# Two weighted sums in another loop order, two half steps of a value projection between three score products, and a key projection cut into a matmul part and a split part

## The chip, the cores and the metric

The kernel runs on 1 core of a Trainium2 chip, as one program. The metric is the device time of one execution in microseconds (us). Three executions of the kernel before took 3112.5, 3117.52 and 3116.73 us; their median is 3116.73 us.

## What is computed

The input is x of shape (4, 256, 64, 64), float32: four images of 256 channels and 4096 points. Two layers follow each other. The reference, cut to what matters here:

```python
# layer 0: self-attention over the 4096 points of an image
q, k, v = wq @ xf + bq, wk @ xf + bk, wv @ xf + bv      # 32, 32 and 256 channels
attn = softmax(q.T @ k);  x = gamma * (v @ attn.T) + x
# layer 1: clustering block
feat, val = conv1x1(group_norm(x), f_w), conv1x1(group_norm(x), v_w)   # 4 heads of 24, 4 folds
sim = sigmoid(beta + alpha * cos(centres, points))       # 4 centres for each fold and head
sim = sim * one_hot(argmax(sim, over the centres))
agg = (sim @ val + pooled val) / (count + 1)             # the weighted sums
y = x + ls1 * conv1x1(agg spread back by sim, proj)
y = y + ls2 * mlp(group_norm(y))                         # 256 -> 1024 -> gelu -> 256
z = relu(bn(conv1x1(relu(bn(y * dw)), pw)))
```

## The kernel before

**Stages.** The images are worked on one after another (b = 0 to 3, line 2061). For each, three functions run: `weighting` (line 958, exponentials and weighted values of the attention, 64 units of 512 keys by 512 queries), `cluster` (line 1141, the clustering block up to the statistics of the second group norm) and `mlp` (line 1639, MLP and pointwise convolution). The scores of the next image's first 8 units are computed inside `cluster` and `mlp` of the present one, so that the next `weighting` can start at once.

**Order of the work.** The program is under a manual schedule: each engine executes its instructions in the order in which the Python code issues them, and semaphores hold an instruction until its inputs are there. TensorE (PE) thus has one hand-written queue, as have VectorE (DVE), ScalarE (ACT), GpSimd (POOL) and the DMA queue on SyncE (SP).

**Fill.** The projections of the next image are cut into a list of small pieces (`parts.projections`, lines 1130 to 1134), each with a size. `fill(n)` (line 2048) pops pieces from this list until their sizes add up to n. It is called at places where PE would otherwise wait. A value piece, `v_step(i, k)` (line 437), has size 1/2 and is one matmul of 128x128 weights by 256 columns, which the hardware executes as two passes. Two values of i share one PSUM buffer of the pool `ps_m`, and the last of their four pieces lets ACT copy the buffer to SBUF (line 451). The list is: values 0 to 13, the first key projection, values 14 to 31, then the second key and the second query projection, each with size 1. That is 35 in sizes. In the first three images the calls to `fill` use up 30 of them before the early scores, 1 and 2 more in the second group norm, so that the second key and query projections are left for `fill(N)` (line 1966), behind the first of the MLP's hidden pieces, `first(0, 0)`.

**Key and query projections.** `halved` (line 425) runs `projected` (line 346: 8 matmuls of 128x32 weights by 512 columns, in turn into the four 32-row quarters of a PSUM buffer), then `halves_of` (line 359), which splits the float32 result into a rounded part (ACT, line 368) and a rest (DVE, line 369), and then sends both to DRAM with four DMAs of SP.

**Early scores.** At the end of `cluster` three units are scored one after another (lines 1516 to 1519). Each `score` (line 539) has four matmuls of 512 columns into two PSUM buffers of the pool `ps_s`, which has just two, and two ACT copies of 128x1024 (line 502).

**Weighted sums.** `summed` (line 1369) is called twice in `cluster`: with the constant `pool_w` as weights (line 1390), and with `sim` as weights (line 1401). Each call has 32 matmuls of 128x32 weights by 96 columns. They go into the four 32-row quarters of one PSUM buffer (q = 0 to 3), and the 8 chunks of points (j) are added up in PSUM. The loop over j is outside, that over q inside, so that consecutive matmuls write four different quarters in turn. Between the two calls stands `fill(5)`, or `fill(4)` in the last image. `weights(0)` and `weights(1)` (line 1285) on DVE write the part of `sim` that belongs to q = 0 and 1, and to q = 2 and 3. Behind the second call come the counts (line 1406), a copy of the sums by ACT (line 1407), transposes (lines 1417 and 1426), the product with the projection (line 1439), and from it the matmuls `op` (line 1461), whose results DVE adds to y (line 1473). DVE then takes the statistics (line 1454), which feed the second group norm.

**Second group norm.** `group_norm` (line 301) has two tiny matmuls (lines 309 and 310), `fill(1)`, a third matmul (line 320), ACT's square root (line 224), a table load for the gelu (line 299), and `fill(counts)`. Its default for `counts` is 2. Then `norm(0)` normalises the first 512 points on DVE (lines 1672 and 1739 to 1742), and `first(0, 0)` starts the MLP on PE (line 1859).

Of the kernel before, what the change touches and what calls it, by code (L numbers as in the profile page):

```python
# [10 lines left out]
AF = mybir.ActivationFunctionType  # L11
# [22 lines left out]
EARLY = 3  # L34
# [26 lines left out]
def attention_then_cluster_block(  # L61
# [235 lines left out]
    def table(f):  # L297

        nc.scalar.activation(probe, probe, f)
# [38 lines left out]
    def attention(b, xs, ys):  # L338
# [7 lines left out]
        def projected(which, i, ps):  # L346

            col = 1 if which == "k" else 0
            for k in range(KC):
                for r in range(RG):  # L350
                    nc.tensor.matmul(
                        ps[r * D : (r + 1) * D],
                        wqk_s[:, k, col],
                        block(xs, k, 4 * i + r),
                        start=(k == 0),
                        stop=(k == KC - 1),
                    )

        def halves_of(which, hi, lo, ps):

            col = 1 if which == "k" else 0
            if which not in own:
                own[which] = dram.tile([NBLK // RG, P, 4, NB], F32, tag=which, name=f"{which}_{b}")
            bias = bqk_s[:, col : col + 1]
            nc.scalar.activation(hi, ps, AF.Identity, bias=bias)
            nc.vector.scalar_tensor_tensor(
                lo, ps, bias, hi.bitcast(F32), ALU.add, ALU.subtract  # L370
            )

        def part_of(which, c, hi, lo):
            return (hi if c in ((0, 2) if which == "k" else (0, 1)) else lo).bitcast(F32)

        def written(which, i, hi, lo, dma=nc.sync):
            rows = own[which][i]
            for c in range(4):
                dma.dma_start(out=rows[:, c], in_=part_of(which, c, hi, lo))
# [42 lines left out]
                ks[u], ks[u + 1] = two[:, 0], two[:, 1]  # L422
            straight("k", u % RG, ks[u], *src)

        def halved(which, i, write=True):

            ps = ps_m.tile([P, NB], F32, tag="m", name=f"{which}p_{b}_{i}")
            two = work.tile([P, 2, NB], F32R, tag="t13", name=f"hl_{which}_{b}_{i}")
            projected(which, i, ps)
            halves_of(which, two[:, 0], two[:, 1], ps)  # L430
            if write:
                written(which, i, two[:, 0], two[:, 1])
            return two[:, 0], two[:, 1]

        vps = {}
# [689 lines left out]
        parts = Parts()  # L1125
# [5 lines left out]
            (1 / KC, lambda i=i, k=k: v_step(i, k)) for i in range(N // P) for k in range(KC)  # L1131
        ]
        parts.projections[14 * KC : 14 * KC] = [(1, lambda: halved("k", 0))]
        parts.projections += [(1, lambda w=w: halved(w, 1)) for w in "kq"]
        parts.queries = lambda: halved("q", 0)
        return parts

# [3 lines left out]
    def cluster(b, ys, stats, cells, rest, fill, gelu, nxt, maxima, turn):  # L1141
# [112 lines left out]
        def similar(f, between=lambda: None):  # L1254

            def meanwhile():
                table(AF.Gelu_apprx_tanh)
                between()

            sg = sgs[f]  # L1260
            rsqrt(prns[f], prns[f], L2_EPS, meanwhile)
            nc.vector.tensor_tensor(quad(sg), quad(sg), over_m(prns[f]), ALU.mult)
            nc.scalar.activation(sg, sg, AF.Tanh, scale=ab[:, 0:1], bias=ab[:, 1:2])
            if f == 0:
                gelu(0)
                table(AF.Sqrt)
# [24 lines left out]
        later = {6: lambda: similar(0)}  # L1291
# [30 lines left out]
        for nb in range(NBLK):  # L1322
# [7 lines left out]
            ps = ps_s.tile([P, 2, 2, C], F32, tag="s", name=f"fv_{b}_{nb}")  # L1330
# [19 lines left out]
            for g in range(2):  # L1350
                q = 2 * fh + g
# [15 lines left out]
        agg_p = ps_a.tile([P, NB], F32, tag="a0", name=f"agg_{b}")  # L1367

        def summed(w, first):
            for j in range(8):  # L1370
                for q in range(4):
                    nc.tensor.matmul(
                        agg_p[q * 32 : (q + 1) * 32, :ED],
                        w(j, q),
                        vf[2 * (q // 2) + j // 4][:, (j // 2) % 2, 2 * (q % 2) + j % 2, ED:],
                        start=(first and j == 0),
                        stop=(not first and j == 7),
                    )
# [70 lines left out]
        stats2 = small.tile([P, 2 * NBLK, 6], F32, tag="stats", bufs=1, name=f"st2_{b}")  # L1449
# [66 lines left out]
        for u in range(EARLY):  # L1516
            copies = []
            nxt.score(u, copies, maxima)
            copies.pop()()
        return stats2  # L1520


# [116 lines left out]
    def mlp(b, ys, stats2, fill, nxt, blocks, turned, maxima):  # L1639
# [16 lines left out]
        w3_s, (pw_bcd, pw_bac, pw_abcd) = few[:, :h_n], (few[:, h_n + i] for i in range(3))  # L1656
        nc.gpsimd.tensor_tensor(w3_s, s2_s, a12_s, ALU.add)
        ga, gb = group_norm(
            b, "gn2", stats2, fill, meanwhile=lambda: table(AF.Gelu_apprx_tanh)
        )  # L1660
        ob = out[b].rearrange("(k p) h w -> p k (h w)", p=P)
        pairs = {}
# [145 lines left out]
        def first(nb, j, todo, slots, meanwhile=lambda: None):  # L1808


            hs = work.tile([P, 2, NB], F32, tag=("t", "acc")[j % 2], bufs=1, name=f"hs_{b}_{nb}_{j}")

            def gelu(i, src):
                nc.scalar.activation(  # L1814
                    src, src, AF.Gelu_apprx_tanh, bias=pvc("b1", P, j + 4 * (i > 1))
                )

            ws = [
                w[:, j * P : (j + 1) * P] for w in (W_A, w_abcd, W_CD, w_bac, w_bcd, W_B, W_D)
            ]  # L1820
            seven(f"{nb}_{j}", ws, pairs[nb][:, 0], pairs[nb][:, 1], quarters(hs), gelu, todo, slots, meanwhile)
            return hs
# [120 lines left out]
        def rest():  # L1943
            if maxima:
                maxima.pop(0)()
# [8 lines left out]
        for nb in range(blocks):  # L1954
            end = nb == blocks - 1
            for j in range(4):
                if j > 1:
                    rest()
                if end and j == 3:

                    rest()
                    rest()
                pw = (lambda: last(nb - 1, True, nc.gpsimd)) if end and j == 2 else lambda: None
                hs = first(nb, j, todo, slots, pw)
                if nb == 0 and j == 0:
                    fill(N)
                if j > 1 or end:
                    rest()
                if nxt and nb:
                    for _ in range(3 if end else 1):  # L1970
                        if nxt.sums:
                            nxt.sums.pop(0)()
                if j == 0:
                    if nb:
                        rectify = finish(nb - 1, acc)
                    acc = [
                        ps_a.tile([P, NB], F32, tag=f"a{c}", name=f"mo{c}_{b}_{nb}")
                        for c in range(KC)
                    ]
                    if not end:  # L1980
                        acc += [
                            ps_m.tile([P, NB], F32, tag="m", name=f"mo{c}_{b}_{nb}")
                            for c in range(2, 4)
                        ]
                    elif nxt:

                        nc.sync.dma_start(
                            out=a21_s, in_=w2.rearrange("(k p) m -> p k m", p=P)[:, :h_n, P:]
                        )
                        nxt.q_block(1)  # L1990
                elif j == 1:
                    assert not drips and not hooks
                    if nb:
                        rectify()
                    if not end:
                        ahead = norm(nb + 1, nc.gpsimd)
                        if nb:
                            own = factors(nc.gpsimd, pairs[nb - 1][:, 1], pairs[nb - 1][:, 0])
                        else:
                            own = left_factors()  # L2000
                elif j == 2 and nb and not end:
                    pointwise(nb - 1)
                scored = nxt and (nb, j) in at
                if scored:
                    copies = []
                    nxt.score(at[nb, j], copies, maxima)
                    copies.pop()()
                if len(acc) == KC:
                    todo = second(nb, acc, hs, j)
                    slots = (2, 1, 0, 1) if scored else (0, 1, 1, 2)  # L2010
                else:
                    todo = second_by_seven(nb, acc, hs, j, own, ahead)
                    slots = (0, 2, 2, 3)
                    if scored:
                        slots = (3, 1, 2, 1)
                    elif j == 2 and nb:
                        slots = (3, 1, 0, 3)
# [38 lines left out]

    with tc.manual_schedule():
        here = attention(0, xs0, [])
        here.alone()
        late = None  # L2060
        for b in range(B):
            xs1 = []
            nxt = attention(b + 1, xs1, []) if b + 1 < B else None
# [10 lines left out]
            fill = filler(todo)  # L2074
# [11 lines left out]
            stats2 = cluster(b, here.ys, stats, cells, rest, fill, gelu, nxt, maxima, turn)  # L2086
# [79 lines left out]
```

## Time and profile before

The profiled execution took 3112.69 us; its span on the core is 3110.9 us. So 1.8 us lie around the span. The mean granted clock of TensorE was 0.998 of full speed.

| engine | busy us | share of the span | instructions |
|---|---|---|---|
| PE (matmul) | 3042.2 | 98% | 14210 |
| PEld (weight load) | 2488.0 | 80% | 14210 |
| DVE | 2501.5 | 80% | 3548 |
| POOL | 2327.7 | 75% | 2243 |
| ACT | 1779.4 | 57% | 2817 |

The span is one sequence of four images of about 760 us each. In the table a matmul counts as busy until its modelled end, and matmuls overlap, so 98% does not say that the array is always at its peak. Timeline rows give the start in us from the beginning of the span, the time from the first start to the last end of a merged group, the engine, the line, the operation, the tiles (out<-in), the shape and the number of instructions; a bracket at the end tells how long the engine idled before, and what ended the idle time. One float32 matmul of the program appears as two matmul records with two weight loads; the two passes are counted one by one in the rows.

### The profile page before, as it was taken

Reading aid. Unit: us, or ns where it says so; the run is one execution under the profiler, and the core shown is the slowest. Engines: PE = TensorE matmul, PEld = TensorE weight load, DVE = VectorE, ACT = ScalarE, POOL = GpSimd, SP = SyncE. Lnnn points to the kernel's source line nnn. Section 1 sums busy time; section 2 is a strip of 40 time slices with the busy share of each in tenths; the row PEclk is TensorE's granted clock in tenths of the full one; section 3 lists DMA queues with packets and bytes.
Section 4 is the critical chain, followed back from the end, with each engine's and each line's share of the span. In section 5 each row is a group of like instructions: output and inputs, shape, how many; then the busy total and the mean of one; then the engine's idle time right before and its main releaser. Section 6 shows DMA issues by size and latency. Waiting matters only on the chain.

```text
span 3110.9 us, 41355 instructions
## 1 busy us (share of the span) xinstructions
PE 3042.2 (98%) x14210; PEld 2488.0 (80%) x14210; DVE 2501.5 (80%) x3548; ACT 1779.4 (57%) x2817; POOL 2327.7 (75%) x2243
## 2 busy tenths in 40 slices
PE   8999999999999999999999999999999999999999
PEld 5788887788688888878868888887877888885886
DVE  4998888777798888877779888877768988887675
ACT  5666664544566666454456666645456666655444
POOL 6888887477588888648758888965766988894563
PEclk9999999999999999999999999999999999999999
DMA  5112226100112113510011222441011212150000
GB/s 175 45 58 65 62 84 176 58 18 28 52 45 68 55 62 108 159 48 28 18 58 45 69 62 65 117 147 35 28 41 48 59 54 68 55 154 2 13 21 28
DMA packets 105570, 200.40 MB, mean 64 GB/s; under 512 B 14880, under 2 KB 30864, under 8 KB 103824
## 3 DMA queue, kind: packets, MB, share of 16 engines
q1 hardware_dynamic: 100464, 178.66, 18.0%
q0 software_dynamic: 4256, 18.90, 2.9%
q8 instruction: 113, 1.85, 0.2%
q14 instruction: 97, 0.79, 0.1%
q10 hardware_dynamic: 640, 0.20, 0.0%
HBM read 147.01 MB, written 48.34 MB: 63 GB/s over the span
## 4 chain that ended last, share of the span: by engine, by line
PE 74%; DVE 9%; POOL 8%; issue 3%; ACT 3%; DMA 2%; SPq 1%; POOLq 0%; ACTq 0%; DVEq 0%
PE av L734 34%; PE mo L1776 10%; PE sc L489 7%; PE hq L1859 5%; PE hp L1859 3%; PE hr L1859 3%; PE fv L1334 3%; POOL acc L664 3%; DVE s L655 2%; POOL t L664 2%; DVE top L513 2%; PE vp L443 1%; POOL s L664 1%; PE mo L1760 1%; DMA w<-in_w 1%
## 5 line engine op out<-in xcount | busy, mean ns | idle before, releaser
L502 ACT COPY s<-sc 128x1024 f32<-128x1024 f32 x512 | 515.1, 1012 | 427.5 <-PE sc L489 419.0
L655 DVE TENSOR_TENSOR s<-s,hold 128x1024 f32<-128x1024 f32 x512 | 598.4, 1209 | 10.7 <-ACT hold L638 5.5
L664 POOL TENSOR_TENSOR acc<-acc,t 128x512 f32<-128x512 f32 x408 | 541.4, 1347 | 0.0
L734 PE MATMUL av<-s,sum 128*128 128x256 f32 x2048 | 526.9, 380 | 3.7 <-POOL s L664 3.5
L734 PE MATMUL av<-t,v 128*128 128x256 f32 x2048 | 527.1, 380 | 2.4 <-POOL t L664 2.2
L734 PE MATMUL av<-s,v 128*128 128x256 f32 x2048 | 525.7, 379 | 2.2 <-ACT xn L1727 1.1
L664 POOL TENSOR_TENSOR s<-t,s 128x512 f32<-128x512 f32 x256 | 340.5, 1330 | 226.3 <-DVE t L678 158.9
L678 DVE TENSOR_TENSOR t<-s,hold 128x1024 f32<-128x1024 f32 x256 | 311.7, 1218 | 189.8 <-POOL acc L664 93.3
L513 DVE TENSOR_TENSOR top<-sc,top 128x1024 f32<-128x1024 f32 x350 | 426.6, 1219 | 21.6 <-ACT s L502 18.0
L734 PEld LDWEIGHTS av<-s,v 128*128 128x128 f32 x2048 | 387.2, 189 | 64.6 <-ACT xn L1727 2.3
L734 PEld LDWEIGHTS av<-t,v 128*128 128x128 f32 x2048 | 387.5, 190 | 63.1 <-POOL t L664 8.4
L734 PEld LDWEIGHTS av<-s,sum 128*128 128x128 f32 x2048 | 387.9, 190 | 61.1 <-POOL s L664 8.6
L1814 ACT ACTIVATE hs<-hs,pv_s 128x256 f32<-128x256 f32 x496 | 232.6, 503 | 352.3 <-DVE hs L1850 352.3
L489 PE MATMUL sc<-q,k 128*128 128x512 f32 x1024 | 391.6, 466 | 22.2 <-ACT s L502 10.5
L1776 PE MATMUL mo<-hs,w 128*128 128x256 f32 x1512 | 384.9, 381 | 0.0
L664 POOL TENSOR_TENSOR t<-s 128x512 f32<-128x512 f32 x256 | 329.8, 1288 | 45.4 <-PE av L734 31.9
L1776 PEld LDWEIGHTS mo<-hs,w 128*128 128x128 f32 x1512 | 283.6, 190 | 47.2 <-ACT hs L1814 6.3
L659 ACT ACTIVATE hold<-s 128x512 f32<-128x512 f32 x256 | 154.2, 602 | 214.4 <-DVE s L655 214.2
L1850 DVE TENSOR_TENSOR hs<-hq,hs 128x256 f32<-128x256 f32 x496 | 198.5, 421 | 85.8 <-PE hq L1859 75.5
L661 ACT ACTIVATE s<-s 128x1024 f32<-128x1024 f32 x256 | 266.9, 1043 | 0.0
L489 PEld LDWEIGHTS sc<-q,k 128*128 128x128 f32 x1024 | 173.7, 189 | 110.9 <-DVE top L513 59.1
L734 PE MATMUL av<-t,sum 128*128 128x256 f32 x1024 | 262.4, 378 | 0.0
(292 smaller groups left out, 4844.2 us busy)
## 6 DMA issues: line engine op xcount, KB each, us to landing
k<-k SPq DMA_DIRECT2D x248, 256.0 KB, 2.7
x<-in_x SPq DMA_DIRECT2D x62, 512.0 KB, 6.8
out<-xn SPq DMA_DIRECT2D x62, 256.0 KB, 2.1
att<-t SPq DMA_DIRECT2D x56, 256.0 KB, 4.0
x<-att POOLq DMA_DIRECT2D x12, 1024.0 KB, 9.7
w<-in_w SPq DMA_DIRECT2D x8, 1024.0 KB, 11.4
q<-q SPq DMA_DIRECT2D x31, 256.0 KB, 4.1
rden<-row_rd SPq DMA_DIRECT2D x28, 256.0 KB, 3.7
```

The costliest lines, as they stand in the source:

```text
L489: nc.tensor.matmul(sc[:, r, :], k_s[:, (2 * h + r) * P : (2 * h + r + 1) * P], qs[u // GRP], start=True, stop=True,)
L502: nc.scalar.copy(slots[u][:, PAIR[h]].rearrange("p h r n -> p r h n"), tiles(sc))
L513: nc.vector.tensor_tensor(top, src, top if saved[nb] is None else saved[nb], ALU.max)
L655: nc.vector.tensor_tensor(sh, sh, mb.to_broadcast([P, 2, 2, QW]), ALU.subtract)
L661: nc.scalar.activation(s[:, PAIR[1]], s[:, PAIR[1]], AF.Exp)
L664: nc.gpsimd.tensor_tensor(out, x, y, op)
L678: nc.vector.tensor_tensor(t31[u], s[:, B11 : B22 + 1 : 2], b12.to_broadcast([P, 2, 2, QW]), ALU.add)
L734: nc.tensor.matmul(av[bank][:, half_ * QW : (half_ + 1) * QW], a[:, r], t[:, r], start=(g == 0 and r == 0 and i in (1, 7, 2, 4)), stop=(g ...
L1776: return nc.tensor.matmul(bank[:, half * HB : (half + 1) * HB], a[:, j], t, start=start, stop=stop)
L1814: nc.scalar.activation(src, src, AF.Gelu_apprx_tanh, bias=pvc("b1", P, j + 4 * (i > 1)))
L1850: nc.vector.tensor_tensor(dst, ps, term, ALU.add)
L1859: nc.tensor.matmul(out, w, x, start=True, stop=True)
```

## The change

The diff in full:

```diff
@@ -422,14 +422,23 @@
+        ripe = []
+
-        def halved(which, i, write=True):
+        def halved(which, i, write=True, later=False):
 
             ps = ps_m.tile([P, NB], F32, tag="m", name=f"{which}p_{b}_{i}")
             two = work.tile([P, 2, NB], F32R, tag="t13", name=f"hl_{which}_{b}_{i}")
             projected(which, i, ps)
-            halves_of(which, two[:, 0], two[:, 1], ps)
-            if write:
-                written(which, i, two[:, 0], two[:, 1])
+
+            def split():
+                halves_of(which, two[:, 0], two[:, 1], ps)
+                if write:
+                    written(which, i, two[:, 0], two[:, 1])
+
+            if later:
+                ripe.append(split)
+            else:
+                split()
             return two[:, 0], two[:, 1]
@@ -1131,7 +1140,8 @@
-        parts.projections += [(1, lambda w=w: halved(w, 1)) for w in "kq"]
+        parts.projections += [(1, lambda w=w: halved(w, 1, later=w == "k")) for w in "kq"]
+        parts.ripe = ripe
@@ -1367,8 +1377,8 @@
         def summed(w, first):
-            for j in range(8):
-                for q in range(4):
+            for q in range(4):
+                for j in range(8):
                     nc.tensor.matmul(
                         agg_p[q * 32 : (q + 1) * 32, :ED],
                         w(j, q),
@@ -1517,6 +1527,8 @@
             copies = []
             nxt.score(u, copies, maxima)
             copies.pop()()
+            if u + 1 < EARLY:
+                fill(0.5)
         return stats2
@@ -1656,7 +1668,12 @@
         ga, gb = group_norm(
-            b, "gn2", stats2, fill, meanwhile=lambda: table(AF.Gelu_apprx_tanh)
+            b,
+            "gn2",
+            stats2,
+            fill,
+            meanwhile=lambda: table(AF.Gelu_apprx_tanh),
+            counts=2,
         )
@@ -1963,6 +1980,8 @@
                 hs = first(nb, j, todo, slots, pw)
                 if nb == 0 and j == 0:
+                    if nxt:
+                        nxt.ripe.pop(0)()
                     fill(N)
```

- **Sums:** in `summed` the loop over the quarter q is now outside and that over the chunk j inside. The 8 matmuls of one quarter follow each other, 16 passes in a row into the same quarter. This holds for both calls in all four images.
- **Half steps:** between the three early scores of the first three images `fill(0.5)` is called twice. It runs the two pieces of value 29, one behind score 0 and one behind score 1; the second of them is followed by ACT's copy of values 28 and 29.
- **Second keys:** the list of pieces is thereby one size further on in the second group norm. Its `fill(1)` runs value 30, and its `fill(2)` value 31 and the matmuls of the second key projection. ACT's and DVE's split of these keys and their four DMAs are put off until behind `first(0, 0)`, where they stood before too. `fill(N)` then has only the second query projection left.
- `counts=2` is what the default gave.

## The prediction

> **What bounds the kernel now.** I read the page first: engine shares and the chain of work that ended last.
>
> ```profile
> PE 3042.2 (98%) x14210; PEld 2488.0 (80%) x14210; DVE 2501.5 (80%) x3548; ACT 1779.4 (57%) x2817; POOL 2327.7 (75%) x2243
> ...
> PE 74%; DVE 9%; POOL 8%; issue 3%; ACT 3%; DMA 2%; SPq 1%; POOLq 0%; ACTq 0%; DVEq 0%
> ```
>
> PE bounds nearly everything, so PE time in a dense stage is paid in full, and whatever moves into a PE wait is free. The change touches some 45 us of each image, where the chain also runs through DVE and ACT. So I took the timeline by engine there. First the weighted sums of image 0: PE, then ACT, then the last image.
>
> ```profile
> 565.11 1.53 PE L1372 MATMUL agg<-vf,pool_w 128*32 128x96 f32 x64
> 566.57 4.58 PE L443 MATMUL vp<-wv_s,x 128*128 128x256 f32 x20
> 571.08 0.36 PE L1372 MATMUL agg<-vf,sim 128*32 128x96 f32 x4
> 572.44 1.51 PE L1372 MATMUL agg<-vf,sim 128*32 128x96 f32 x60 [1.00 <-DVE sim L1287]
> ...
> 574.10 0.60 PE L1417 MATMUL tp<-ident,sim 128*128 128x128 f32 x4
> ```
> ```profile
> 574.00 0.24 ACT L1407 COPY scr<-agg 128x96 f32<-128x96 f32 x1 [1.58 <-PE agg L1372]
> ```
> ```profile
> 2848.46 1.86 PE L1372 MATMUL agg<-vf,sim 128*32 128x96 f32 x64
> ```
>
> Each sum is 64 passes. PE runs the first, then fill, then 4 passes of the second (q = 0 and 1 of the first chunk), then waits 1.00 us for `weights(1)`. ACT waits for the end of the sum. Then DVE:
>
> ```profile
> 578.17 2.73 DVE L1473 SCALAR_TENSOR_TENSOR x<-op,pc_s,x 128x512 f32<-128x512 f32 x4 [2.45 <-PE op L1461]
> 580.81 2.46 DVE L1454 BATCH_NORM_STATS2 st<-x 128x6 f32<-128x512 f32 x4
> 583.19 2.71 DVE L1473 SCALAR_TENSOR_TENSOR x<-op,pc_s,x 128x512 f32<-128x512 f32 x4
> 585.82 7.20 DVE L1454 BATCH_NORM_STATS2 st<-x 128x6 f32<-128x512 f32 x12
> 593.05 0.59 DVE L307 BATCH_NORM_AGGREGATE mv_gn<-st 128x2 f32<-128x96 f32 x1
> ```
>
> From 578.17 to 593.64 DVE has no gap, and it began because PE's `op` came, which hangs on the sum by way of ACT's copy. So a sum that ends later delays the group norm, and with it the MLP, one to one. Last, the scores, the norm and the start of the MLP, on PE and ACT:
>
> ```profile
> 588.29 1.28 PE L489 MATMUL sc<-q,k 128*128 128x512 f32 x4
> 590.21 0.74 PE L489 MATMUL sc<-q,k 128*128 128x512 f32 x2 [0.63 <-ACT s L502]
> 591.12 0.74 PE L489 MATMUL sc<-q,k 128*128 128x512 f32 x2 [0.18 <-ACT s L502]
> 592.42 1.28 PE L489 MATMUL sc<-q,k 128*128 128x512 f32 x4 [0.55 <-DMA k<-k]
> ...
> 597.67 0.67 PE L1859 MATMUL hp<-xn,w 128*128 128x256 f32 x2 [0.44 <-ACT probe L299]
> 599.09 0.67 PE L1859 MATMUL hp<-xn,w_abcd 128*128 128x256 f32 x2 [0.75 <-DVE xn L1740]
> ...
> 601.85 1.92 PE L351 MATMUL kp<-x,wqk_s 128*32 128x512 f32 x16
> 603.59 1.90 PE L351 MATMUL qp<-x,wqk_s 128*32 128x512 f32 x16
> ```
> ```profile
> 595.31 0.58 ACT L451 COPY v<-vp 128x512 f32<-128x512 f32 x1 [0.23 <-PE vp L443]
> 595.79 0.27 ACT L224 ACTIVATE rstd_gn<-gnv_gn,eps 128x1 f32<-128x1 f32 x1
> ```
>
> PE idles 0.63 and 0.55 us between scores and 0.44 and 0.75 us before the MLP; the second keys (kp) stand behind that, in dense PE time. Images 1 and 2 show the same rows within 0.15 us.
>
> **Part 1, the sums.** How long is one pass? The 128-column passes of `tp` last 272 ns each by their median duration, and four fit in 0.60 us, so one starts every (600 - 272)/3 = 109 ns, all into the whole array. A 96-column pass then needs 96/128 of it, 82 ns. But the 64 passes of a sum (246 ns each) start every (1530 - 246)/63 = 20.4 ns, a quarter of 82. So four passes run side by side, one for each quarter q, and the loop with q inside is what offers four different quarters in turn. Even the two passes of one matmul do not hold up the next quarter. In the new order 16 passes into one quarter come in a row.
>
> The trace has no such sequence, so I bound it. Let S be the time from the first pass of a sum to the instruction behind it. Today S is 566.57 - 565.11 = 1.46, of which 0.18 lies behind the last start. **Lower end:** PE looks far enough ahead to run all quarters at once, and S stays 1.46. **Upper end:** a weight load (110 ns in the rows of line 1372) stands bare in each step: 63 x 0.110 + 0.18 = 7.1. **Value taken:** one pass every 82 ns, as each quarter does today with its weight loads hidden, and one pass of overlap at each of the three changes of quarter: 60 x 0.082 + 0.18 = 5.10. It is nearest to the rows: they show that PE passes over one waiting pass of a quarter, and nothing shows more than a few.
>
> PE's order is sum, fill, sum. The first sum moves fill by S - 1.46. The second began at 571.08 and the next matmul (counts) at 573.88, so it took 2.80 with its wait; the new one starts 3.64 later, at 574.7, with `sim` complete since 572.4, and takes S. The early start of q = 0 and 1 before `weights(1)`, which the new order offers, thus gains nothing at this S. Per image (S - 1.46) + (S - 2.80); in the last one, where the sum ran without the long wait (2848.46 to 2850.26), (S - 1.46) + (S - 1.80). Over four images: 8S - 16.0. With 5.10: **+24.8 us**, all on the path by the DVE chain above.
>
> The page "TensorE: Matmul & The Clock Gate" of the Trainium skill, Part 3, says that matmuls of small M run concurrently if their outputs lie in different 32-partition strips; the 20.4 ns agree, and it speaks against this change. Part 2 of the same page says that matmuls stay in program order and only weight loads are pulled ahead; strictly taken this gives 63 x 82 ns, S = 5.35 and +26.8 us, and it does not fit a trace in which the second pass of a quarter does not hold up the next quarter.
>
> **Part 2, the half steps (three images).** Two passes of 256 columns take 4.51 us / 20 x 2 = 0.45 us. Behind score 0 they lie in the 0.63 us wait for ACT, behind score 1 in the 0.55 us wait for the key DMA: nothing on the path. Without that cover they would cost 0.9 us per image. Value 29 leaves the norm's `fill(1)`, but value 30 takes its place, so the third matmul stays at 595.11. ACT's copy of values 28 and 29 (0.58) now stands ahead of score 2's copies and pushes these some 0.3 us, to about 595.4; nobody waits for them but buffers wanted at 597. In return it is gone from in front of the square root, which starts at 595.42 instead of 595.79: **-0.37 us**, and the reciprocal, DVE's norm and the MLP's second product (599.09) follow. If the cover fails there, nothing is gained.
>
> **Part 3, the second keys (three images).** kp runs 601.85 to 603.59, 1.74 us of dense PE time. Now it stands in the norm: value 31 (0.87) from 595.25, a switch of array tiling of 0.1 (as between `hr` and kp today), kp 1.74, so PE is free at about 598.0. The first product of the MLP starts there instead of at 597.67, and ends its 0.5 us before the second one's input, at 599.09 - 0.37 = 598.7. So kp is wholly covered by the idle time and by value 29 being gone: **-1.74 us**. If that cover were gone it would cost as much again. Its PSUM buffer is now held some 8 us longer, but the next to want that pool are the query projection (other buffer) and later the MLP's accumulators, in the same order as before. ACT's (0.67) and DVE's (0.75) split and SP's four DMAs are issued where they were, ahead of the query's; ACT and DVE reach them at about the old time, and the MLP behind is PE-bound. So what PE gains it keeps.
>
> Per image -2.1, three images **-6.3 us**. `counts=2` changes nothing.
>
> **Sum:** 8S - 16.0 - 6.3 = 8S - 22.3; with S = 5.10, **+18.5 us**. On the profiled execution, 3112.69 (1.8 around its span), that is 3131.2. The median of the runs shown is 4 us higher, and the four executions known lie in two pairs around 3114.9; I put the forecast on that middle: **3133 us**.
>
> **Rivals.** (1) *PE keeps the quarters side by side* in the new order, because its queue looks past 16 waiting passes. For it: the queue already passes over a waiting pass. Against: that is one pass per quarter, not sixteen. With S = 1.46, or 1.6 with a late start of the last quarter, the second sum still ends about where it does, since q = 2 and 3 wait for `weights(1)` until 572.4. Then only parts 2 and 3 count: -5 to -6.3 us, 3109, not slower. It decides from S below 2.79, where 8S - 22.3 is nil. (2) *Two quarters at a time*: S = 31 x 0.082 + 0.18 = 2.72, net -0.5, 3114; with S between 2.4 and 3.5, -3 to +6. (3) *Weight loads come bare*, or kp isn't covered (+5.2): S up to 7.1 gives +34.5, 3149. Against: each quarter today reloads its weights every 82 ns. A further few us can come from the clock: in the last image PE waited 3.44 us before the norm, and two 512-column passes behind that took 2.05 us, where two ahead took 1.02; a shift of that stage can lengthen or shorten it.
>
> **How the numbers follow.** Forecast (S 4.3 to 5.4, +12 to +21): 0.62. Rival 1: 0.16, half of it beyond 0.2%. Rival 2: 0.15. Rival 3: 0.07. About 0.2% (6.2 us) is what a measurement of this kernel can tell from no change. So faster 0.08, same 0.23, slower 0.69. Range: it leaves out rival 1 and the far part of rival 3; from rival 2 (-3) to a bare weight load in part (+27): 3112 to 3142.
>
> **What would show it.** In the timeline after, the 64 passes with `pool_w` should last about 5.2 us instead of 1.53, the wait of 1.00 us before `sim` should be gone, and ACT's wait before line 1407 should be longer. The rows of kp should stand between value 31 and the first `hp`, PE's waits of 0.44 and 0.75 should be near 0.1, and ACT's square root should follow score 2's copy at once. If the `pool_w` row stays near 1.5 us, part 1 is wrong and rival 1 holds; if it is near 2.7, rival 2. If kp stands right but `hp` with `w_abcd` comes later against the third matmul of the norm than 4.0 us, part 3 isn't covered.

## The result, and the profile after

The changed kernel took 3128.75 us in the median of five executions (3127.46 to 3131.73), the kernel before 3116.17 us in five (3112.5 to 3117.52). The ratio is 1.0048 with a 95% interval of 1.0038 to 1.0059: slower by half a per cent, or 12.6 us between the medians, where the forecast median was 3133 us. The profiled execution after took 3127.87 us with a span of 3126.1, which is 15.2 us more than the span before.

The weighted sums of image 0, in PE's timeline after (line 1382 is the old 1372):

```profile
563.96 4.57 PE L1382 MATMUL agg<-vf,pool_w 128*32 128x96 f32 x64
568.45 4.58 PE L452 MATMUL vp<-wv_s,x 128*128 128x256 f32 x20
572.97 4.57 PE L1382 MATMUL agg<-vf,sim 128*32 128x96 f32 x64
```

Both sums take 4.57 us now. The second has lost its 1.00 us wait, but it starts 3.04 us later, counted from the start of the first, and takes longer: from the first pass to the next instruction S is 4.50 us in all eight sums, where the first had 1.46 and the second 2.80, its wait included. ACT, which copies the sums, waits 3.26 us for them instead of 1.58:

```profile
577.57 0.24 ACT L1417 COPY scr<-agg 128x96 f32<-128x96 f32 x1 [3.26 <-PE agg L1382]
```

Scores, norm and start of the MLP, PE after (kp and qp are the second key and query projection, `hp` the first products of the MLP):

```profile
593.78 0.73 PE L498 MATMUL sc<-q,k 128*128 128x512 f32 x2 [0.20 <-ACT s L511]
...
599.87 1.92 PE L351 MATMUL kp<-x,wqk_s 128*32 128x512 f32 x16
601.73 0.70 PE L1876 MATMUL hp<-xn,w 128*128 128x256 f32 x2
602.68 0.67 PE L1876 MATMUL hp<-xn,w_abcd 128*128 128x256 f32 x2 [0.25 <-DVE xn L1757]
...
605.44 1.92 PE L351 MATMUL qp<-x,wqk_s 128*32 128x512 f32 x16
```

kp stands between value 31 and `hp`, the waits of 0.44 and 0.75 us have shrunk to 0.25, and behind `first(0, 0)` (the MLP's first piece) qp stands alone.

The two traces set side by side at fixed points (the start of the first sum; the instruction behind the second sum, `cnt`; the start of the MLP's second piece, its first `hp`) tell where the 15.2 us came from. Here are the second and third point of image 0, before and after:

```profile
573.88 0.38 PE L1406 MATMUL cnt<-scr,ones 128*96 128x64 f32 x2
...
605.42 0.70 PE L1859 MATMUL hp<-xn,w 128*128 128x256 f32 x2
```
```profile
577.47 0.38 PE L1416 MATMUL cnt<-scr,ones 128*96 128x64 f32 x2
...
607.29 0.70 PE L1876 MATMUL hp<-xn,w 128*128 128x256 f32 x2
```

Each entry is the growth of the distance between two such points, in us, taken from the starts in ns:

| | image 0 | 1 | 2 | 3 | sum |
|---|---|---|---|---|---|
| both sums and the fill between | 4.73 | 4.74 | 4.74 | 5.74 | 19.95 |
| end of the sums to the MLP's second piece | -1.71 | -1.73 | -1.72 | -0.20 | -5.4 |
| first group norm of the last image | | | | 1.69 | 1.7 |
| everything else, mostly the first 60 us of the program | | | | | -1.1 |

The third row is no effect of the edits in that place; it is the clock. Nor is the last row: in the ten traces of this document the first 55 us of the program, which no edit touches, differ by over 2 us from one to another. Now the clock. These rows give a stretch, its length, the busy time of PE, PEld, DVE, ACT and POOL (with instruction counts), the granted TensorE clock, and last the DMA share and GB/s. Before, and after, at the same place of the work:

```profile
2810.00:2817.00 7.00, 6.90 (x29) 3.65 (x28) 5.00 (x19) 3.35 (x6) 0.00 (x0) 1.00 0.00 0
```
```profile
2818.00:2825.00 7.00, 7.00 (x20) 3.36 (x19) 3.72 (x16) 2.07 (x4) 0.00 (x0) 0.76 0.00 0
```

In both executions PE waits 1.9 us just ahead of this stretch. After, the clock then stood at a half for 3.41 us, which cost 1.69 us; before, it did not.

### The profile page after: what moved, and what is told of

Its sections match the earlier page's. It is cut to its first block, busy times and chain, and to the rows that moved or that the text cites. A ratio compares the mean times of both kernels' runs of the same rounds, so it can differ in the third digit from the quotient of the medians.

```text
span 3126.1 us, 41356 instructions
## 1 busy us (share of the span) xinstructions
PE 3066.6 (98%) x14210; PEld 2515.6 (80%) x14210; DVE 2503.7 (80%) x3548; ACT 1778.5 (57%) x2817; POOL 2327.7 (74%) x2243
## 4 chain that ended last, share of the span: by engine, by line
PE 75%; DVE 8%; POOL 8%; ACT 3%; issue 3%; DMA 2%; SPq 0%; ACTq 0%; POOLq 0%; DVEq 0%
PE av L743 34%; PE mo L1793 10%; PE sc L498 7%; PE hq L1876 5%; PE hp L1876 3%; PE hr L1876 3%; PE fv L1344 3%; POOL acc L673 2%; PE vp L452 2%; DVE top L522 2%; DVE s L664 2%; POOL t L673 1%; PE mo L1777 1%; DMA w<-in_w 1%; POOL s L673 1%
## 5 line engine op out<-in xcount | busy, mean ns | idle before, releaser
L664 DVE TENSOR_TENSOR s<-s,hold 128x1024 f32<-128x1024 f32 x512 | 598.8, 1210 | 10.8 <-ACT hold L647 5.9
```

What stands on the lines that cost most here:

```text
L664: nc.vector.tensor_tensor(sh, sh, mb.to_broadcast([P, 2, 2, QW]), ALU.subtract)
```

## The experiments

Each kernel was run beside the kernel before on the same chip. The medians of before are 3113.89 us for sums_alone, no_sums, half_steps and orders, and 3113.14 us for the others; they differ from the median above, so the ratios are what to compare.

**sums_alone.** The kernel before, with this one edit:

```diff
-            for j in range(8):
-                for q in range(4):
+            for q in range(4):
+                for j in range(8):
```

> The kernel before with the sums' new loop order alone. Theory A (the three parts add up; a sum takes S = 4.50 us in the new order, as the trace after shows, and all of it is on the path): 8 x 4.50 - 16.0 = +19.9 us on before, about 3136, S = 4.50 in all eight sums, ACT's wait before line 1407 about 3.3 us. A further +1.7 if the half clock of the trace after also falls into the last image's first norm. Rival R (keys and half steps gain nothing, the sums' price is the whole difference): +12 to +15 us, about 3130.

3137.16 us, ratio 1.0072 (1.0058 to 1.0085): +23 us. The sums cost what they cost in the full change: S = 4.50 in all eight, and between the start of the first and the end of the second sum 4.73, 4.74, 4.74 and 5.74 us more, 19.95 in all.

```profile
566.24 4.57 PE L1372 MATMUL agg<-vf,pool_w 128*32 128x96 f32 x64
570.74 4.58 PE L443 MATMUL vp<-wv_s,x 128*128 128x256 f32 x20
575.25 4.57 PE L1372 MATMUL agg<-vf,sim 128*32 128x96 f32 x64
```

The span is 24.7 us longer than before. Most of the rest lies in the last image's first norm, where this execution ran at half clock for two windows (6.83 us) and lost 3.36 us:

```profile
2824.50:2831.50 7.00, 6.87 (x13) 3.73 (x14) 3.12 (x12) 0.95 (x2) 0.00 (x0) 0.52 0.00 0
```

So the sums alone explain more than the whole slowdown, and theory R falls.

**no_sums.** The changed kernel, with the sums in their old order (the edit above, undone).

> The changed kernel with the sums' old loop order: half steps and keys alone. Theory A: the trace after shows 1.70 us won per image between the sums and the MLP's second piece, three images, so -5.1 us on before, about 3111; the sums at 1.46 again. Rival R: no difference from before (within 1 us). A third possibility, that parts 2 and 3 reach the forecast -6.3 once the sums don't disturb them: -6.3.

3110.41 us, ratio 0.9989 (0.998 to 0.9997). The stage from the sums to the MLP's second piece is shorter by 1.70, 1.73 and 1.71 us, as in the full change to 0.01 us, together -5.1. The median is 3.5 us below before. The profiled execution lost 1.69 us to a half clock in the last image's first norm; that the others did too isn't shown. The parts add up in their stages. The medians don't: 23.3 - 3.5 is 19.8, where the full change has 12.6. In the spans of the three profiled executions (+24.7, -2.6 and +15.2) the gap is 6.8 us; of these, 4.1 lie in the two group norms of the last image, where the clock differs, and 2.7 in what comes before image 0's sums.

**half_steps.** The kernel before, with the two `fill(0.5)` and one piece less in the norm, so that keys and queries stay where they were:

```diff
+            if u + 1 < EARLY:
+                fill(0.5)
...
             meanwhile=lambda: table(AF.Gelu_apprx_tanh),
+            counts=1,
```

> The kernel before with the half steps alone: the two pieces of value 29 between the scores, and the norm's second fill one piece shorter, so that keys and queries stay together behind the first MLP piece as before. Theory A: ACT's square root comes 0.37 us earlier, but DVE's next operation (line 326) waits for POOL's sum of weights (line 1657), which ends when it did, so nothing is won: within 1 us of before, DVE's line 326 at 0.8 us instead of 0.43. Rival: the square root's 0.37 us is won in three images, -1.1 us, and DVE's line 326 stays at 0.43.

3114.01 us, ratio 1.0002 (0.9993 to 1.001): nothing. The three images' stages differ by at most 0.02 us. ACT's square root does start earlier, but DVE's line 326 takes 0.80 to 0.82 us instead of 0.43 to 0.45. PE's wait in front of the MLP, 0.44 us before, has become 1.32 us: value 29 (0.87 us) no longer stands there:

```profile
601.75 0.67 PE L1876 MATMUL hp<-xn,w 128*128 128x256 f32 x2 [1.32 <-ACT v L460]
603.17 0.67 PE L1876 MATMUL hp<-xn,w_abcd 128*128 128x256 f32 x2 [0.75 <-DVE xn L1757]
```

So the half steps by themselves only move an idle time of PE to where the keys can use it. The keys without the half steps were not run; what of the 1.7 us they would win alone stays open.

**early_w3.** As no_sums, with POOL's last sum of MLP weights (`w3_s`, line 1657) issued behind the clustering's second sum:

```diff
+        sum_w2()        # in cluster, ahead of the memset of line 1428
         nc.gpsimd.memset(agg, 0.0)
...
-        nc.gpsimd.tensor_tensor(w3_s, s2_s, a12_s, ALU.add)     # in mlp
```

> Keys and half steps with the sums in their old order (as no_sums), and POOL's last sum of MLP weights (line 1657) issued some 20 us earlier, in a stretch where POOL idles, so that POOL is done before DVE's line 326. Theory P (DVE's 128x2 operation there waits for POOL's running operation: it ended 23 to 31 ns after POOL's in all executions so far): line 326 takes 0.23 us instead of 0.81, the norm is 0.58 us earlier, of which PE can use some 0.4 before the first MLP product binds; 3 x 0.4 = -1.2 us more than no_sums, -6.3 on before in all. Rival (the long line 326 comes from ACT's table load, which runs at the same time, or from something else): line 326 stays at 0.8, no difference from no_sums.

3105.29 us, ratio 0.9974 (0.9964 to 0.9985): faster than both kernels, 7.9 us below before. First DVE's line 326 and POOL's operation beside it, before, and the same pair in the full change:

```profile
596.29 0.43 DVE L326 TENSOR_SCALAR ga_gn<-pc_s,rstd_gn 128x2 f32<-128x2 f32 x1
```
```profile
595.43 1.26 POOL L1657 TENSOR_TENSOR w<-w,w 128x512 f32<-128x512 f32 x1
```
```profile
599.50 0.81 DVE L326 TENSOR_SCALAR ga_gn<-pc_s,rstd_gn 128x2 f32<-128x2 f32 x1
```
```profile
599.01 1.27 POOL L1669 TENSOR_TENSOR w<-w,w 128x512 f32<-128x512 f32 x1
```

Before, POOL ends at 596.69 and DVE at 596.72; after, POOL at 600.28 and DVE at 600.31. With POOL's operation out of the way:

```profile
595.76 0.23 DVE L326 TENSOR_SCALAR ga_gn<-pc_s,rstd_gn 128x2 f32<-128x2 f32 x1
```
```profile
597.99 0.70 PE L1876 MATMUL hp<-xn,w 128*128 128x256 f32 x2
598.53 0.59 PE L1876 MATMUL hp<-xn,w_abcd 128*128 128x256 f32 x2
```

The operation itself takes 0.23 us; the rest of the 0.43 and 0.81 was waiting for POOL. `hp` now runs without a wait, and theory P holds. The first three images win 0.48 to 0.50 us each by this, 1.5 in all, where 1.2 was expected. The gain over no_sums is larger still by three things: each image gained 0.12 to 0.14 us at the wait for `sim`, the last image 0.94 us between its sums and the MLP's second piece (its cause is open), and this execution had no half clock in the last image's first norm.

**both_keys_queries.** As early_w3, with `fill(6)` for `fill(5)` between the sums and `later=True` for keys and queries.

> As early_w3, and one value more (0.87 us) in PE's 1.00 us wait for sim, so that the second query projection moves into the norm beside the keys, both split behind the MLP's first piece. Theory A (work moved into a PE wait is free, work beyond the wait is paid): 0.87 us of the wait at sim is used; in the norm PE has 3.6 us of projections from 595.3 on instead of 2.6, some 1.1 us more than the norm lets it hide, so of 1.74 won 1.1 is paid back: -0.6 per image, -1.9 us more than early_w3, about -8 on before. Rival (both splits at once hold up ACT and DVE in the MLP's second piece, or the longer wait for the first product isn't made good): no better than early_w3, or slower by up to 2 us.

3104.8 us, ratio 0.9973 (0.9962 to 0.9984): no better than early_w3 that could be told. From the first sum to the MLP's second piece the images won 2.35, 2.37 and 2.36 us; in early_w3 they won 2.33, 2.35 and 2.31. The 0.87 us at `sim` was won, and kp and qp ran in the norm back to back. But the MLP's second piece then found its buffers still in DVE's hands (`hr` are the last products of the first piece):

```profile
602.58 1.03 PE L1876 MATMUL hr<-xn,w 128*128 128x256 f32 x4
604.51 0.70 PE L1876 MATMUL hp<-xn,w 128*128 128x256 f32 x2 [0.90 <-DVE hs L1867]
```

The query projection had covered DVE's work on the first piece. Moved away, it leaves a wait of 0.90 us, which with the later `hp` eats the gain. The rival holds.

**split_at_once.** As no_sums, with the keys split where they are projected (`later=False`).

> As no_sums, but the keys in the norm are split at once, not behind the MLP's first piece. Tells what putting off the split is worth. Theory A: DVE's part of the split (0.75 us) stands ahead of DVE's norm in the queue and waits for kp on PE (done 2.6 us behind the norm's third matmul) and ACT's part (0.67), so the norm starts some 2.5 us later: +2 to +3 us per image against no_sums, +1 to +4 us on before in all. Rival (the split finds room on ACT and DVE): as no_sums, -5.

3124.43 us, ratio 1.0037 (1.0023 to 1.0051): +11 us, more than expected. Image 2 shows the mechanism alone: its stage is 1.45 us longer than before, 3.2 us longer than in no_sums. PE waits 2.62 us in front of the MLP. Images 0 and 1 have the same wait, and there the clock fell as well, so that they lost 4.31 and 3.12 us. Here is image 0 (0.57 of the clock), then image 2 (full clock):

```profile
601.00:609.00 8.00, 7.09 (x22) 4.49 (x26) 4.95 (x13) 1.77 (x5) 0.00 (x0) 0.57 0.27 97
...
2144.00:2152.00 8.00, 6.07 (x34) 3.62 (x35) 5.77 (x16) 2.57 (x6) 0.00 (x0) 1.00 0.36 133
```

Putting off the split is what makes the move of the keys a gain: it avoids a wait of 3.12 us on DVE's queue, and with it the half clock that followed PE's 2.62 us wait in two of the three images. The last image's first norm cost another 3.37 us here.

**orders and fours.** How far does PE look? The kernel before, with other orders in `summed`:

```diff
+            # orders, pool_w: two chunks of a quarter, then the next quarter
+            order = [(2 * i + n, q) for i in range(4) for q in range(4) for n in range(2)]
+            # orders, sim: two quarters in turn, then the other two
+            order = [(j, 2 * h + n) for h in range(2) for j in range(8) for n in range(2)]
+            # fours, pool_w: four chunks of a quarter, then the next quarter
+            order = [(4 * i + n, q) for i in range(2) for q in range(4) for n in range(4)]
```

> The kernel before with two other orders: in the sum with pool_w two chunks of a quarter follow each other (4 passes), then the next quarter, all four in turn; in the sum with sim two quarters take turns for all chunks, then the other two. Tells what limits how far PE looks past waiting passes; the new order overlapped 4 passes at each change of quarter, that is up to 3 waiting passes. Theory Q (each quarter has room for 3 waiting passes of its own): all four quarters run side by side in pool_w, S about 1.5; two side by side in the last image's sim sum, S about 2.45. Theory W (3 waiting passes for all quarters together): pool_w S about 1.75, last sim sum about 2.6. Theory O (strict order of matmuls): pool_w S about 4.7, sim about 2.7 to 5. Whole kernel under Q or W: +1 to +4 us on before.

> The kernel before with four chunks of a quarter in a row (8 passes) in the sum with pool_w, then the next quarter, twice through all four. If each quarter has room for one running and three waiting passes, each quarter's turn overlaps the next one's by four passes: 36 rounds of 82 ns, S = 35 x 0.0825 + 0.02 + 0.18 = 3.1 us. If the room were one waiting pass, S = 4.8; if eight or more, S = 1.5.

Last image of orders, then image 0 of fours:

```profile
2845.23 1.60 PE L1376 MATMUL agg<-vf,pool_w 128*32 128x96 f32 x64
...
2850.39 2.54 PE L1376 MATMUL agg<-vf,sim 128*32 128x96 f32 x64
```
```profile
566.22 3.37 PE L1375 MATMUL agg<-vf,pool_w 128*32 128x96 f32 x64
```

S is 1.53 and 2.47 in orders, which is theory Q (1.5 and 2.45) and not W (1.75 and 2.6). Fours has S = 3.30 where one running and three waiting passes per quarter gave 3.1, one waiting pass 4.8, and eight 1.5. The 0.2 us that are left are the changes of quarter: at each of the seven the step from start to start is 112 ns instead of 82. So with 4 passes of a quarter in a row 0.07 us is lost, with 8 the sum takes 2.3 times as long, with 16 3.1 times. The whole kernels do not contradict this: orders ratio 1.0005 (0.9996 to 1.0015), which can't be told from no change, and fours 3116.4 us in a single execution.

## Why the prediction was right, and where its terms were off

- **Direction and sum.** +18.5 us was forecast against the profiled execution and 15.2 measured; 8S - 16.0 gives 20.0 with the measured S, and the eight sums measured 19.95. That it all lies on the path, by ACT's copy and the gapless DVE chain, held to 0.01 us in each of the first three images: the distance from the end of the sums to the norm's third matmul is what it was. That the two parts outside the sum, +1.69 us of the clock and -1.1 us of "everything else", nearly cancel is luck.
- **Mis-sized term: the overlap at a change of quarter.** The prediction let one pass of a quarter overlap the next one, 60 x 0.082 + 0.18 = 5.10. The trace after shows twelve passes of a quarter alone (starts at 0, 106, 189 to 931 ns), then its last four beside the first four of the next quarter (1014 and 1020, 1096 and 1126, 1179 and 1210, 1261 and 1291 ns): 51 steps from start to start instead of 60, most of them of 82 ns and three of 113 at the changes, S = 4.50. So passes do not start strictly in the order of PE's queue, as the section on the kernel before has it for all instructions. The overlap took 4.8 us off the forecast. The step of 82 ns, with the weight loads hidden, was right. Passes that start strictly in order would give S = 5.10 here if the first pass of a quarter may run beside the last one of the quarter before, 5.35 if it may not, and about 4.7 in the first sum of orders (theory O); 4.50 and 1.53 were measured. The page "TensorE: Matmul & The Clock Gate" of the Trainium skill, Part 2, says that matmuls stay in program order; these traces do not agree with it.
- **The half steps' -0.37 us per image failed.** The square root came 0.37 us earlier as forecast, but the step "the reciprocal, DVE's norm and the MLP's second product follow" was wrong: DVE's line 326 ended with POOL's operation, 0.02 to 0.03 us behind it, in both kernels. The 0.43 us of that 128x2 operation, beside 0.22 for the next one of its size, could have told it in the profile before. early_w3 shows it by taking POOL's operation away.
- **The keys' -1.74 us held** (-1.71 to -1.73, together with half steps that win nothing alone). PE was free for `hp` 3.04 us behind the norm's third matmul, forecast 2.9, and the second product came 3.99 us behind it, 3.98 before. The cover was enough: PE still waits 0.25 us between the two products, where near 0.1 was forecast, because the norm did not come 0.37 us earlier. That the split would cost nothing where it was put held too, and split_at_once shows what it would have cost in the norm.
- **The clock** was named as an uncertainty of a few us in the last image's norm. It came in that image's other norm, +1.69 us.
- Of the rivals, 1 and 2 asked for more than ten passes to be looked past; PE looks past three in each quarter. Rival 3 asked for bare weight loads, and the steps stayed at 82 ns.

The early start of half the second sum, before `weights(1)`, was worth nothing, since the first sum's growth had already used up the 1.00 us wait. And in the old order the four quarters run abreast, so that the remainder behind `weights(1)` takes 1.27 us to its last start; that is about the 15 steps of 82 ns that a single quarter's 16 passes need anyway. As no run shows a quarter taking passes faster, an estimate from these rows is that no order of these passes can be much shorter there.

## What to carry to other kernels

Where matmuls with few output rows go to different 32-row quarters of the output, their order in the program is their parallelism: go round all four quarters, with at most four passes, two float32 matmuls, in a row into one. Two quarters in turn are not enough: the last image's second sum of orders then took 2.47 us. A piece of matmul work moved into a wait of PE pays in full if what follows it on other engines is left where it was; but look at what that piece covered in its old place. And if a tiny DVE operation takes two to four times its usual time, look at what POOL is doing at its end.

## What the runs showed of the hardware that was not expected

- PE looks past up to three waiting passes in each of the four quarters, each quarter for itself (S = 1.53, 2.47, 3.30 and 4.50 us for four orders of the same 64 passes). Only passes of 96 columns were tried, always two to a matmul, so whether passes or matmuls count is open.
- A 128x2 operation of DVE with two operands per partition from small tiles took 0.23 us alone, and 0.34 to 0.99 us beside a running POOL addition; in the twenty cases beside POOL in the traces of before, after, no_sums, half_steps and sums_alone it ended 22 to 29 ns behind a POOL operation. Not every small operation waits so: in the trace before, DVE's 128x1 operations of lines 314 and 317 took 0.22 and 0.14 us in the middle of POOL's line 1654.
- The granted clock fell to a half for one or two windows of 3.41 us behind some PE waits of 1.9 to 2.6 us and not behind others of the same length; behind the 3.44 us wait in the last image's second norm it fell in all ten traces. It cost 1.69 or 3.37 us in the last image's first norm, and some 2.9 and 1.7 us in images 0 and 1 of split_at_once. Which wait is hit changes from trace to trace; this alone moves such a kernel by a few us. Why a given wait is hit stays open.
